# Attention over hyperedges: the feature sums of two chunks, and their use, in every second turn of the loop

## The chip, the core and the metric

The kernel runs on one core of one Trainium2 chip. A core has engines that run side by side, each with its own list of instructions that it works off in order: TensorE (PE in the profile; its weight loads are PEld), VectorE (DVE), ScalarE (ACT), GpSimd (POOL) and SyncE (SP), which here only issues transfers. An instruction that needs another engine's result waits on a semaphore, and everything behind it on the same engine waits too. The metric is the time of one execution on the device in microseconds (us), lower is better; given is the median of several runs.

## The reference, cut to what matters

Four graph layers run one after the other on x, 8 batches of 2048 nodes with 64 features. The change lies at the end of the first of them, where two candidates for a node, `industry` (from the adjacency matrix) and `g` (from the hyperedges), are weighed against each other and added to x:

```python
def attn_scores(f):
    return jnp.tanh(f @ fcW + fcb) @ av
...
industry = jnp.einsum('nm,bmf->bnf', adj / deg, x @ W_ind)
...
g = jnp.einsum('bne,benf->bnf', coefs1, all_he)
pair = jnp.stack([industry, g], axis=2)
coefs2 = jax.nn.softmax(attn_scores(pair), axis=-1)
out = jnp.einsum('bnk,bnkf->bnf', coefs2, pair)
...
# --- layer 0 (adj_preln) ---
h = jnp.maximum(_layernorm(x, axis=-1), 0.0)
x = x + _L0_gnn_ref(h, ...)
# --- layer 1 (adj_preln) ---
h = jnp.maximum(_layernorm(x, axis=-1), 0.0)
x = x + _L1_gnn_ref(h, adj, L1_gnn_W, L1_gnn_a)
```

A softmax over two scores is a sigmoid of their difference. So with d = score(industry) - score(g) the layer's output is g + (1 + tanh(d/2)) * (industry - g)/2, and that is how the kernel computes it.

## The kernel before, in words

The data lie transposed: two batches of 64 features fill the 128 partitions (a pair p, four of them), the 2048 nodes lie along the free axis in four chunks of 512. The stage of the change works through 4 pairs x 4 chunks = 16 chunks, numbered 0 to 15 (lines 1506 to 1592). Chunks 0 to 3 are pair 0, 4 to 7 pair 1, and so on. For each chunk i there are these steps:

- `fetch(i)`, line 1520: SP loads 256 KB of `industry` (half of it, already scaled) from DRAM into one of 8 buffers `iv`. It may only start when the buffer's last user, eight chunks earlier, is done.
- `first(i)` and `second(i)`, lines 1525 and 1528, both through `scores`, line 1509: TensorE multiplies the chunk of `iv`, or of `gT` (whose tiles are called `hn` in the profile), by fcW into a `pf` tile, one matmul per batch (two records each). There are two `pf` tiles. ScalarE takes the tanh into a `th_s` tile of 128x1024; six of these come from a pool named `pt`. `second` also has VectorE turn `iv` into (industry - g)/2 in place. That instruction overwrites what `first(i)` reads, so it waits for `first(i)` on TensorE.
- `differ(i)`, line 1534: VectorE subtracts the two tanh tiles, 128x1024.
- `third(i)`, line 1537: TensorE sums that difference over the features with weights av, one matmul per batch, into a `pd` tile; there are two of these. ScalarE takes the tanh in place. These are the feature sums of the title.
- `fourth(i)`, line 1545: VectorE computes (tanh + 1) * iv. For pair 0 it also adds g and x (two more instructions) and SP stores the result; for the other pairs GpSimd issues a transfer that adds the tile onto DRAM. After the last chunk of a pair, `late_tile` has GpSimd load one more megabyte of the adjacency matrix.

The turn i of the loop (line 1572) issues, in this order, `first(i+1)`, `second(i+1)`, `third(i-1)`, `differ(i)`, `fourth(i-2)`, `fetch(i+6)`; ahead of it stand `fetch(0)` to `fetch(6)`, `first(0)`, `first(1)` and `second(0)`. Between them `near(engine, i)` issues the steps that prepare pair 0 for the next layer's attention, by a plan that is written out by hand (`first_neighbours`, lines 1667 to 1794): in turns 4 to 8 and again 8 to 12 means, a layer norm and a projection (`mean`, `xc`, `q`, `ph`, `hS`, `raw`), in turns 12 to 14 a Newton iteration in small VectorE instructions, in turns 14 and 15 the spread of scores over partitions (`pb`, `R`), in turns 16 and 17 the first four `pt` tiles of the attention. The wrappers `V`, `A`, `G`, `S` and `kit.strict` keep the order of issue on each engine as the program has it.

The next layer's attention follows at once (`attend`, line 1821): VectorE makes two `pt` tiles of 128x1024 for each of 16 blocks of nodes, and TensorE multiplies them (`o`, `dn`).

Of the kernel before, what the change touches and what calls it, by code (L numbers as in the profile page):

```python
# [27 lines left out]
def half(b2):  # L28
    return slice(b2 * 64, (b2 + 1) * 64)


def cols(c, w=CW):
    return slice(c * w, (c + 1) * w)
# [603 lines left out]
class Kit:  # L637
# [97 lines left out]
    def mm(self, *args, **kw):  # L735

        one = self.nc.tensor.matmul(*args, **kw)  # L737
        if self.strict:
            self.tc.keep_in_program_order(one)
# [36 lines left out]
def layer0(kit, hn, x1_dram, open_early, late_tile, between):  # L776
# [542 lines left out]
    with ExitStack() as s0:  # L1319
# [125 lines left out]
        for j in range(last + 2 * NB):  # L1445
            i, k = divmod(j, NB)
# [55 lines left out]
    with ExitStack() as s0:  # L1502
        io = s0.enter_context(tc.tile_pool(name="o_io", bufs=1, reuse_waits="tile"))
        sb = s0.enter_context(tc.tile_pool(name="o_sb", bufs=2, reuse_waits="tile"))
        ps = s0.enter_context(tc.tile_pool(name="o_ps", bufs=2, space=PSUM, reuse_waits="tile"))
        chunks = [(p, c) for p in range(NP) for c in range(NCW)]
        ivs, ths, tgs, ccs, xs = {}, {}, {}, {}, []

        def scores(v, f):

            act = A if kit.strict else nc.scalar
            pf = ps.tile([P, 2, CW], FP, tag="pf", name="pf")
            for b2 in range(2):
                kit.strict = kit.strict or b2 == 1
                mm(pf[:, b2, :], fcW[half(b2), :], v[half(b2), :], start=True, stop=True)
            th = one.pt.tile([P, HN], FP, tag="pt", name="th_s").rearrange("p (b n) -> p b n", b=2)
            act.activation(th, pf, AF.Tanh, bias=fcb, scale=f)
            return th

        def fetch(i):  # L1520
            p, c = chunks[i]
            ivs[i] = io.tile([P, CW], FP, tag=f"iv{i % 8}", name="iv")
            S.dma_start(out=ivs[i], in_=ind_dram[p, :, cols(c)])

        def first(i):
            ths[i] = scores(ivs[i], 2.0)

        def second(i):
            p, c = chunks[i]
            tgs[i] = scores(gT[p][:, cols(c)], 1.0)  # L1530

            V.scalar_tensor_tensor(ivs[i], gT[p][:, cols(c)], -0.5, ivs[i], op0=OP.mult, op1=OP.add)

        def differ(i):
            V.tensor_sub(ths[i], ths[i], tgs.pop(i))

        def third(i):
            pd = ps.tile([P, CW], FP, tag="pd", name="pd")
            th = ths.pop(i)
            for b2 in range(2):  # L1540
                mm(pd[half(b2), :], Av, th[:, b2], start=True, stop=True)
            A.activation(pd, pd, AF.Tanh, scale=0.5)
            ccs[i] = pd

        def fourth(i):
            p, c = chunks[i]
            df = ivs.pop(i)
            V.scalar_tensor_tensor(df, ccs.pop(i), 1.0, df, op0=OP.add, op1=OP.mult)
            if p:
                G.dma_start(out=x1_dram[p, :, cols(c)], in_=df, accum_op=OP.add)  # L1550
            else:
                V.tensor_add(df, df, gT[p][:, cols(c)])
                V.tensor_add(xs[c], xs[c], df)
                nc.sync.dma_start(out=x1_dram[p, :, cols(c)], in_=xs[c])
            if c == NCW - 1:
                late_tile(p)

        G = InOrder(tc, nc.gpsimd)
        for i in range(5):
            fetch(i)  # L1560
        for c in range(NCW):
            xs.append(sb.tile([P, CW], FP, tag="x", name="xo", bufs=NCW))
            S.dma_start(out=xs[c], in_=t["xT"][0, :, cols(c)])
            if c < 2:
                fetch(5 + c)
        first(0)
        kit.strict = False
        first(1)
        second(0)
        near = one.first_neighbours(xs, V, A)  # L1570

        for i in range(len(chunks) + 2):
            near("DVE", i)
            if 0 < i < len(chunks) - 1:
                first(i + 1)
            if i < len(chunks) - 1:
                second(i + 1)
            near("PE0", i)
            if 0 < i <= len(chunks):
                third(i - 1)  # L1580
            near("PE", i)
            if i < len(chunks):
                differ(i)
            if i > 1:
                fourth(i - 2)
            if 0 < i and i + 6 < len(chunks):
                fetch(i + 6)
            near("V2", i)
            near("ACT", i)
            if i in (3, 7, 11):  # L1590
                p = 1 + i // 4
                G.dma_start(out=x1_dram[p], in_=gT[p], accum_op=OP.add)
# [721 lines left out]
def four_layers(  # L2314
# [13 lines left out]
    with ExitStack() as s:  # L2328
# [20 lines left out]
        def between(_):  # L2349
            ahead.append(Layer1(kit, x1, aT))  # L2350
            return ahead[0]

        layer0(kit, hn, x1, early, late_tile, between)
        later = []

# [56 lines left out]
```

## Time and profile before

| what | value |
|---|---|
| median of 3 runs | 1859.51 us (1858.75 to 1859.87) |
| the profiled execution: its own time | 1860.53 us |
| its span, first to last instruction | 1858.7 us |
| mean granted TensorE clock | 0.994 of full speed |
| first `pf` matmul of the stage | at 351.09 us |
| last `fourth` of the stage on VectorE | 420.99 to 421.67 us |
| 16 `differ` on VectorE | 1212 to 1225 ns each |
| 32 tanh of `scores` on ScalarE | 1106 to 1121 ns each |
| 64 `pd` matmul records of `third` | 592 to 643 ns each |
| 64 `pf<-iv` matmul records of `first` | 589 to 693 ns each |

The table has rows of the page and of the answers on single tiles. Times are counted from the start of the span. Records of TensorE overlap: two matmuls on different rows or columns of the array run at once, and the next starts while the last drains, so a record's duration is longer than the distance to the next one. In a row of the timeline the bracket at the end is the idle time of that engine just before the row, and what ended it.

### The profile page before, as it was taken

The page shows a single profiled execution, that of the slowest core. Times are in us where ns is not written, and L with a number is a line of the kernel's source. Part 1 is how long each engine was busy: PE and PEld are TensorE (multiplying, and loading weights), DVE is VectorE, ACT ScalarE, POOL GpSimd, SP SyncE. Part 2 cuts the span into 40 slices and gives each one's busy share as a digit, 9 for nine tenths or more (in the row PEclk, how much of TensorE's full clock was granted, in tenths as well). Part 3 has the DMA queues.
Part 4 walks back from the last instruction along what each step waited for, and adds up shares of the span by engine and source line. Part 5 has one row for each costly group of instructions (what it writes and reads, how often), then busy time and mean ns, then how long its engine had stood idle before and what let it go on. Part 6 is the DMA issues. An engine that isn't in the chain of part 4 may idle for free.

```text
span 1858.7 us, 26259 instructions
## 1 busy us (share of the span) xinstructions
PE 1819.8 (98%) x10358; PEld 1139.3 (61%) x10358; DVE 1196.4 (64%) x1881; ACT 474.6 (26%) x1085; POOL 315.9 (17%) x437
## 2 busy tenths in 40 slices
PE   8999999899999999999999999999999999999997
PEld 7878767343333333467765577855687755777653
DVE  7778799789999998942346822357523277424465
ACT  5433455572222221121311112301112101113000
POOL 3212487120000000000112200012100021101122
PEclk9999999999999999999999999999999999999998
DMA  6677494492222222142101022100122011221000
GB/s 193 175 214 217 126 283 120 114 213 75 59 54 52 64 58 58 46 94 74 51 5 36 22 69 63 35 24 22 48 63 63 12 28 32 61 58 51 5 20 13
DMA packets 84389, 142.61 MB, mean 77 GB/s; under 512 B 31752, under 2 KB 32008, under 8 KB 81520
## 3 DMA queue, kind: packets, MB, share of 16 engines
q1 hardware_dynamic: 62832, 79.59, 14.6%
q0 software_dynamic: 21200, 58.03, 12.8%
q10 hardware_dynamic: 224, 3.22, 0.5%
q8 instruction: 83, 1.36, 0.3%
q14 instruction: 50, 0.41, 0.1%
HBM read 106.85 MB, written 37.09 MB: 77 GB/s over the span
## 4 chain that ended last, share of the span: by engine, by line
PE 49%; issue 10%; DMA 2%; POOL 2%; DVE 1%; POOLq 0%; ACT 0%; SPq 0%; DVEq 0%
PE acc L737 31%; PE u L737 14%; PE py L737 2%; PE pv L737 1%; PE tv L744 1%; PE tx L744 1%; POOL fold L2298 1%; DMA den<-d_dram 0%; DMA xd<-e 0%; DMA d_dram<-ds 0%; DMA W3f<-in_L_gnn_weight 0%; PE tp L744 0%; POOL ot L2299 0%; DVE pt L1813 0%; POOL ot L2300 0%
## 5 line engine op out<-in xcount | busy, mean ns | idle before, releaser
L737 PE MATMUL acc<-aT,parts 128*128 128x512 f32 x1664 | 432.1, 404 | 0.0
L737 PEld LDWEIGHTS acc<-aT,parts 128*128 128x128 f32 x1664 | 305.2, 188 | 81.8 <-issue 23.1
L737 PE MATMUL o<-pt,hS 128*32 128x512 f32 x2048 | 247.5, 593 | 2.9 <-DVE pt L1813 1.6
L2286 DVE TENSOR_TENSOR pr<-u,embf 128x512 f32<-128x512 f32 x256 | 170.6, 687 | 120.6 <-PE u L737 114.0
L737 PE MATMUL u<-W3f,y 64*128 64x512 f32 x1024 | 241.3, 589 | 0.0
L1813 DVE SCALAR_TENSOR_TENSOR pt<-R,wd,aT 128x1024 f32<-128x1024 f32 x188 | 230.1, 1277 | 8.0 <-DMA R<-r_dram 5.7
L737 PEld LDWEIGHTS u<-W3f,y 64*128 64x128 f32 x1024 | 100.1, 187 | 119.6 <-issue 119.6
L737 PEld LDWEIGHTS o<-pt,hS 128*32 128x32 f32 x2048 | 75.0, 110 | 149.2 <-issue 124.3
L737 PE MATMUL dn<-pt,vd 128*32 128x512 f32 x1024 | 135.0, 593 | 0.0
L737 PE MATMUL u<-W3f,v 64*128 64x512 f32 x512 | 133.1, 596 | 0.0
L2298 POOL TENSOR_TENSOR fold<-fold 128x256 f32<-128x256 f32 x64 | 47.7, 746 | 477.0 <-DVE fold L2297 477.0
L2066 DVE TENSOR_TENSOR yb<-py,cb_f 128x512 f32<-128x512 f32 x32 | 22.1, 692 | 152.6 <-PE py L737 152.6
L1106 PE MATMUL acc<-at,Y 128*128 128x512 f32 x384 | 103.3, 405 | 0.0
L737 PE MATMUL acc<-aTl,parts 128*128 128x512 f32 x384 | 97.5, 396 | 0.0
L2175 POOL TENSOR_TENSOR bq<-bq,xp 128x512 f32<-128x512 f32 x16 | 20.6, 1288 | 423.0 <-ACT xp L2088 423.0
L2290 DVE TENSOR_TENSOR pr<-pr 128x512 f32<-128x512 f32 x128 | 88.0, 688 | 2.2
L737 PEld LDWEIGHTS u<-W3f,v 64*128 64x128 f32 x512 | 56.5, 186 | 48.6 <-issue 35.7
L1813 DVE SCALAR_TENSOR_TENSOR pt<-R,wd,aTl 128x1024 f32<-128x1024 f32 x64 | 79.3, 1280 | 8.7 <-PE dn L737 3.9
L737 PEld LDWEIGHTS acc<-aTl,parts 128*128 128x128 f32 x384 | 72.1, 188 | 17.0
L737 PEld LDWEIGHTS dn<-pt,vd 128*32 128x32 f32 x1024 | 38.2, 110 | 70.3 <-issue 55.6
L1106 PEld LDWEIGHTS acc<-at,Y 128*128 128x128 f32 x384 | 68.8, 188 | 12.7 <-issue 0.3
L2080 DVE TENSOR_TENSOR parts<-tp,parts 128x512 fp32r<-128x512 f32 x16 | 11.1, 691 | 85.2 <-ACT parts L2079 85.2
(372 smaller groups left out, 2709.8 us busy)
## 6 DMA issues: line engine op xcount, KB each, us to landing
at<-in_adjT POOLq DMA_DIRECT2D x32, 512.0 KB, 5.3
raw<-in_adjT SPq DMA_DIRECT2D x64, 256.0 KB, 3.4
aT<-in_adjT POOLq DMA_DIRECT2D x12, 1024.0 KB, 7.5
xp<-xd SPq DMA_DIRECT2D x45, 256.0 KB, 3.0
R<-r_dram SPq DMA_DIRECT2D x14, 512.0 KB, 3.7
hhi<-hi_dram POOLq DMA_DIRECT2D x18, 235.1 KB, 4.4
hlo<-lo_dram POOLq DMA_DIRECT2D x18, 235.1 KB, 4.6
hi_dram<-hi SPq DMA_DIRECT2D x16, 264.0 KB, 2.9
```

The costliest lines, as they stand in the source:

```text
L737: one = self.nc.tensor.matmul(*args, **kw)
L744: one = self.nc.tensor.transpose(dst, src, self.ident[0:k, 0:k])
L1106: mm(acc[p], Y[h][:, m, p, :], at[:, k, :], start=m + h == 0, stop=m == NT - 1 and h == 1)
L1813: V.scalar_tensor_tensor(pt, R, w, a.bitcast(FP), op0=OP.max, op1=OP.mult)
L2066: nc.vector.tensor_tensor(yb, py, bias[:, None, :].to_broadcast([P, 4, P]), op=OP.add)
L2080: nc.vector.tensor_tensor(lo, tp, hi.bitcast(FP), op=OP.subtract)
L2175: nc.gpsimd.tensor_add(bq, bq, xp)
L2286: nc.vector.tensor_tensor(a, u[h], emb[:, i, 8 * w : 8 * w + 8, None].to_broadcast([P, 8, F]), op=OP.mult)
L2290: nc.vector.tensor_add(pr[h], pr[h], a)
L2298: nc.gpsimd.tensor_add(fold[:, :, 0:2, :], fold[:, :, 0:2, :], fold[:, :, 2:4, :])
```

## The change

The loop's order is changed, and nothing else. `third` and `fourth` are issued for two chunks together in every even turn from 2 to 16, `third` now at the head of the turn ahead of `first(i+1)` and `second(i+1)`, and `fourth` at its old place after `differ(i)`. The loads are issued two at a time in the odd turns.

```diff
         for i in range(len(chunks) + 2):
             near("DVE", i)
+            if i and i % 2 == 0 and i <= len(chunks):
+                third(i - 2)
+                third(i - 1)
             if 0 < i < len(chunks) - 1:
                 first(i + 1)
             if i < len(chunks) - 1:
                 second(i + 1)
             near("PE0", i)
-            if 0 < i <= len(chunks):
-                third(i - 1)
             near("PE", i)
             if i < len(chunks):
                 differ(i)
-            if i > 1:
+            if i > 1 and i % 2 == 0:
                 fourth(i - 2)
-            if 0 < i and i + 6 < len(chunks):
-                fetch(i + 6)
+                fourth(i - 1)
+            for k in (i + 5, i + 6):
+                if i % 2 and 6 < k < len(chunks):
+                    fetch(k)
             near("V2", i)
             near("ACT", i)
             if i in (3, 7, 11):
```

Every chunk is still computed by the same instructions on the same engines. For an even chunk, `third` comes one turn later than before and `fourth` in the same turn; for an odd chunk, `third` comes in the same turn but ahead of the turn's other matmuls, and `fourth` one turn earlier. `fetch(7)` stays in turn 1, odd ones stay in their turns, and `fetch(8)`, `fetch(10)`, `fetch(12)` and `fetch(14)` move from the even turn to the odd one after it.

## The prediction

> **What bounds the kernel now.** I read the page first, then the busy time by stretches, then the timelines of TensorE and VectorE in the stage, each for its idle brackets.
>
> ```profile
> PE 1819.8 (98%) x10358; PEld 1139.3 (61%) x10358; DVE 1196.4 (64%) x1881; ACT 474.6 (26%) x1085; POOL 315.9 (17%) x437
> ```
>
> Over the whole span TensorE looks like the bound. But a share over stages with different limits does not price an edit in one of them, so I look at the stage (351 to 422 us) and at what follows.
>
> ```profile
> 420.00:430.00 10.00, 10.00 (x94) 3.56 (x89) 10.00 (x12) 1.95 (x3) 1.43 (x2) 1.00 0.74 181
> 470.00:700.00 230.00, 230.00 (x2108) 73.62 (x2104) 214.70 (x189) 53.09 (x160) 13.83 (x20) 1.00 0.23 56
> ```
>
> The columns are the stretch, its length, then busy time (instructions) of PE, PEld, DVE, ACT and POOL, the granted clock, DMA share and GB/s. Behind the stage VectorE is busy without a break (10.00 of 10.00) and then for 93% of the time. So a microsecond by which VectorE leaves the stage later is a microsecond at the end. VectorE's instructions in the stage are the same before and after; what can change is only how long it stands idle among them.
>
> ```profile
> 360.09 0.69 DVE L632 SCALAR_TENSOR_TENSOR iv<-hn,iv 128x512 f32<-128x512 f32 x1 [1.24 <-PE pf L737]
> 360.70 1.22 DVE L632 TENSOR_TENSOR th_s<-th_s 128x1024 f32<-128x1024 f32 x1
> 361.83 0.68 DVE L632 SCALAR_TENSOR_TENSOR iv<-pd,iv 128x512 f32<-128x512 f32 x1
> 362.55 0.69 DVE L632 TENSOR_TENSOR iv<-iv,hn 128x512 f32<-128x512 f32 x1
> 363.27 0.69 DVE L632 TENSOR_TENSOR xo<-xo,iv 128x512 f32<-128x512 f32 x1
> 363.89 0.68 DVE L632 SCALAR_TENSOR_TENSOR iv<-hn,iv 128x512 f32<-128x512 f32 x1
> ...
> 402.18 0.69 DVE L632 SCALAR_TENSOR_TENSOR iv<-hn,iv 128x512 f32<-128x512 f32 x1 [0.48 <-PE pf L737]
> 402.79 1.22 DVE L632 TENSOR_TENSOR th_s<-th_s 128x1024 f32<-128x1024 f32 x1
> 403.92 0.68 DVE L632 SCALAR_TENSOR_TENSOR iv<-pd,iv 128x512 f32<-128x512 f32 x1
> 404.52 0.17 DVE L632 TENSOR_SCALAR varn<-raw 128x32 f32<-128x32 f32 x1
> ...
> 407.35 0.68 DVE L632 SCALAR_TENSOR_TENSOR iv<-hn,iv 128x512 f32<-128x512 f32 x1
> ```
>
> This is VectorE's timeline. From start to start: the half-difference in `second` 0.61 us, `differ` 1.13, `fourth` 0.60, or 2.06 for pair 0 with its two additions. A turn of pair 0 is 3.80 (360.09 to 363.89). From 357 us, where the loop runs evenly, to 421.6 VectorE's brackets add up to 8.9 us: 1.24 early, then 2.04 in turns 7 and 8, 1.78 in turns 9 and 10, 3.01 in turns 11 and 12, 0.84 in turns 16 and 17.
>
> ```profile
> 401.00 1.13 PE L737 MATMUL pf<-iv,fcWf 64*128 64x512 f32 x4
> 401.96 1.02 PE L737 MATMUL pf<-hn,fcWf 64*128 64x512 f32 x4
> 402.92 1.08 PE L737 MATMUL pd<-th_s,Avf 128*64 128x512 f32 x4
> 403.93 1.13 PE L737 MATMUL pf<-iv,fcWf 64*128 64x512 f32 x4
> ...
> 414.66 1.94 PE L737 MATMUL pd<-th_s,Avf 128*64 128x512 f32 x8
> 416.53 1.05 PE L737 MATMUL o<-pt,hS 128*32 128x512 f32 x4
> ```
>
> TensorE's blocks follow each other by 0.96 (`first`), 0.96 (`second`) and 1.01 (`third`), 2.93 a turn. Its brackets between 351 and 422 add up to 4.1 us. So the stage is in balance: for pair 0 VectorE is slower (3.80 against 2.93), later TensorE. Neither stops the other for long, because `third(i-1)` has two other blocks (1.92 us) in front of it in its turn, during which VectorE can finish `differ(i-1)` and go on.
>
> **The change, part by part.** *Two blocks of `third` together.* Two apart take 2.02 (twice 1.01), two together 1.87 (414.66 to 416.53), so 0.15 is saved. `first` and `second` of two chunks now follow each other too; I give that 0.2, the two places where a 0.96 block is longer than the two 0.43 steps inside it. That is 0.35 a pair of chunks, 2.8 us for eight, and it counts only where TensorE sets the pace.
>
> *`third` ahead of `first` and `second`.* This is the new wait. In an even turn TensorE's list is `third(i-2)`, `third(i-1)`, `first(i+1)`. `third(i-1)` needs `differ(i-1)`, VectorE's last instruction of the turn before. Queued behind it on TensorE are `first(i+1)` and `second(i+1)`. VectorE's next instruction, the half-difference of `second(i+1)`, waits for `first(i+1)`, and behind that stand `differ(i)` and both `fourth`. So in every even turn VectorE finishes `differ(i-1)`, then waits for a round trip: 0.1 until TensorE starts, 1.01 for `third(i-1)`, 1.18 from the start of `first` to the instruction that waits for it (401.00 to 402.18): 2.3 us. The 1.92 us of cover is gone.
>
> Turn by turn, VectorE's stops: turns 2 and 4, nothing in front: 2.3 each. Turns 6 and 10: one clip of 0.3 from the neighbour plan fills part: 2.0 each. Turns 8 and 12: VectorE already waits there for projections (2.04 and 3.01 before). The new stop costs at least its 2.3 with the old ones inside it, at most 2.0 + 2.3 = 4.3; TensorE has two more blocks of `ph` of 1.87 each to run there, so I take 3.8. Turn 14: 0.8 of `rstd` and `hS` fill: 1.5. Turn 16: there is no `first`, but `fourth(15)` now stands before three `pt` and waits for its tanh: the old 0.84 and one more tanh step of 0.5, 1.3. Sum 19.0, against 8.9 before: **+10.1 us**; with the bounds for turns 8 and 12, +7.1 to +11.1.
>
> *`fourth` for two chunks.* Same instructions; for pair 0 they form a block of 4.1 us in turns 2 and 4, in front of the next `differ`. That makes a long stop on TensorE. After VectorE starts `second(3)` it needs 0.61 + 1.13 + 4.12 + 0.61 + 1.22 + 0.05 = 7.7 us until `third(3)` may start; TensorE meanwhile has 0.74 left of `second(3)`, 1.92 for chunk 4, 1.01 for `third(2)` and some 0.5 of waiting for a `pf` tile: 4.2. It stands 3.5 us. The same holds in turn 5, and in turn 13, where the Newton chain (404.52 to 407.35, 2.8 us) stands in front of `differ(13)`. These stops are part of VectorE's ledger above, but they touch the clock:
>
> ```profile
> 343.17 2.02 PE L737 MATMUL pgs<-mix,S 128*114 128x512 f32 x2 [3.37 <-DVE gn L632]
> ```
>
> ```profile
> 342.00:346.00 4.00, 2.83 (x8) 1.70 (x9) 1.62 (x3) 0.01 (x1) 0.00 (x0) 0.54 0.00 0
> 346.00:350.00 4.00, 3.70 (x8) 1.45 (x6) 0.26 (x1) 2.07 (x8) 0.00 (x0) 0.61 0.00 0
> ```
>
> The one stop of that length inside this kernel, 3.37 us before 343.17, is followed by 6.8 us at about half clock (0.54 and 0.61 in the two stretches). A round trip at half clock costs 2.2 more (1.01 + 1.18 again). With three stops that is 0 (no drop) to 6.6 (three drops on the path); a drop can begin too early or too late for the round trip, so I take half: **+3.3**.
>
> [...]
>
> *Loads two at a time.* Four loads start a turn later, none adds bytes. The work that hides them: `fetch(8)` landed 3.1 us after its issue at 364.41, its chunk was read at 378.80. The late ones wait anyway until the transfer that adds the buffer's old chunk to DRAM has landed (5 to 10 us). `fetch(12)` was issued at 385.96, took 9.5 and was read at 396.19, 0.7 us to spare. As the stage stretches, its reader moves back about as far as the load. I cost it at 0; without that cover each microsecond late is one on TensorE, at most some 2 per load. GpSimd's list keeps its order. ScalarE's work is 2.5 us a turn (twice 1.01 and 0.52), below TensorE's, in the new order too.
>
> The sum against the profiled span is 1858.7 + 13.4 = 1872.1. The median lies 0.8 above that span, so the time is 1859.5 + 13.4 = 1872.9.
>
> **The rivals.** *No clock drop, the round trips alone:* 1859.5 + 10.1 = 1869.6, down to 1866.6 if turns 8 and 12 hide more. For it: the stops are barely as long as the one that dropped. Against: there are three of them.
>
> *Faster: TensorE sets the pace.* If VectorE runs far enough ahead that `differ(i-1)` is always done, the 2.8 us saved on TensorE are the whole effect: 1856.7. For it: 98% busy, and 4.1 us of idle in the stage. Against: the half-difference cannot run ahead of `first`, and `differ(i-1)` stands behind it. It decides if the stops of the even turns stay under 1.1 us on average (8.9 over eight).
>
> *The loads come late.* With readers in pairs, chunks 12 and 14 could wait 2 us each, on top of the main case: 1877.
>
> *Absorbed, no change:* a later wait takes up the delay. Against: VectorE's waits between 418 and 480 us add up to 5 us only, so at most 5 of the 13 could vanish. It takes halved round trips as well.
>
> **How the numbers follow.** Round trips with clock drops 0.53, between 1870 and 1877; without drops 0.24; loads late 0.10; faster 0.06; no change 0.07. The predicted time is the first case's, 1873 rounded. The range takes the first two cases and the lower half of the loads: 1866 (+7.1) to 1878 (10.1 + 1.0 + 6.6 = +17.7, rounded up). About what a measurement can tell from no change is 0.2%, 3.7 us: faster 0.06, same 0.07, slower 0.87.
>
> **What would show it.** In the changed profile VectorE's `iv<-hn,iv` of odd chunks should carry brackets of about 2.3 us from PE `pf`, those of even chunks none. TensorE's `pd` rows should come as x8 or in twos, with waits of some 3.5 us for VectorE in turns 4, 6 and 14. The first `o` of the attention should start 10 to 14 us later, the granted clock should dip in the stage, and everything behind it should keep its length. I am wrong if the brackets are short, if TensorE shows no stops, or if the attention starts late and still ends on time.

## The result, and the profile after

The changed kernel takes 1874.41 us (median of 6 runs, 1871.80 to 1876.07), against 1858.90 us of six runs of the kernel before beside it: a ratio of 1.0082, with a 95% interval of 1.0072 to 1.0092. It is slower by 15.5 us; forecast were 13.4.

The profiled execution has a span of 1874.3 us, which is 15.6 more than before. The page's first part shows where it is not:

```profile
PE 1827.3 (97%) x10358; PEld 1143.0 (61%) x10358; DVE 1196.5 (64%) x1881; ACT 475.2 (25%) x1085; POOL 315.9 (17%) x437
```

VectorE is busy for as long as before (1196.4 there), with as many instructions. TensorE is busy 7.5 us longer with the same 10358 matmuls: some of them ran longer. Now the stage, from near its first matmul to near its end, and the 264 us behind it. First the changed kernel, then the kernel before; the columns are those of the prediction (the stretch, its length, busy time of PE, PEld, DVE, ACT and POOL, granted clock, DMA share, GB/s).

```profile
352.00:436.00 84.00, 71.70 (x316) 28.65 (x316) 56.98 (x91) 51.59 (x69) 15.32 (x19) 0.90 0.69 153
436.00:700.00 264.00, 263.83 (x2400) 85.64 (x2396) 244.10 (x219) 66.47 (x206) 13.82 (x20) 1.00 0.24 61
```

```profile
352.00:422.00 70.00, 65.92 (x330) 27.44 (x330) 57.50 (x92) 51.10 (x70) 14.07 (x18) 1.00 0.81 183
422.00:686.00 264.00, 263.37 (x2400) 85.79 (x2396) 245.08 (x219) 66.70 (x206) 15.22 (x22) 1.00 0.24 61
```

The stage is longer, VectorE does the same work in it, and the granted clock fell from 1.00 to 0.90. In the 264 us behind it the same 2400 matmuls run as before. Counted exactly, from the start of the first `pf` to the end of the fourth `pt` on VectorE, the stage went from 69.98 to 85.64 us (+15.66), and what lies behind it from 1437.7 to 1437.9. So the whole loss arose in the stage and arrived at the end in full. (One `fourth` of 0.60 us stands behind that point in the kernel before and ahead of it in the changed one; more on it below.)

VectorE's timeline shows in which turns. The rows are the half-difference in `second`, with the bracket that says how long VectorE stood idle before it, and one `differ` between them:

```profile
360.76 0.69 DVE L632 SCALAR_TENSOR_TENSOR iv<-hn,iv 128x512 f32<-128x512 f32 x1 [2.24 <-PE pf L737]
...
366.61 0.68 DVE L632 SCALAR_TENSOR_TENSOR iv<-hn,iv 128x512 f32<-128x512 f32 x1
367.21 1.22 DVE L632 TENSOR_TENSOR th_s<-th_s 128x1024 f32<-128x1024 f32 x1
372.51 0.69 DVE L632 SCALAR_TENSOR_TENSOR iv<-hn,iv 128x512 f32<-128x512 f32 x1 [4.09 <-PE pf L737]
...
385.23 0.69 DVE L632 SCALAR_TENSOR_TENSOR iv<-hn,iv 128x512 f32<-128x512 f32 x1 [3.52 <-PE pf L737]
...
394.70 0.69 DVE L632 SCALAR_TENSOR_TENSOR iv<-hn,iv 128x512 f32<-128x512 f32 x1 [2.35 <-PE pf L737]
...
424.07 0.69 DVE L632 SCALAR_TENSOR_TENSOR iv<-hn,iv 128x512 f32<-128x512 f32 x1 [3.25 <-PE pf L737]
```

These are odd chunks: VectorE waits for `first` in every even turn. The half-differences of even chunks, such as the one at 366.61, have no bracket. TensorE's timeline over the same turns shows the other half of the round trip:

```profile
363.99 1.08 PE L737 MATMUL pd<-th_s,Avf 128*64 128x512 f32 x4
368.48 1.98 PE L737 MATMUL pd<-th_s,Avf 128*64 128x512 f32 x4 [3.41 <-DVE th_s L632]
370.38 2.08 PE L737 MATMUL pf<-iv,fcWf 64*128 64x512 f32 x4
372.25 1.92 PE L737 MATMUL pf<-hn,fcWf 64*128 64x512 f32 x4
...
420.04 1.97 PE L737 MATMUL pd<-th_s,Avf 128*64 128x512 f32 x4 [3.31 <-DVE th_s L632]
421.94 2.08 PE L737 MATMUL pf<-iv,fcWf 64*128 64x512 f32 x4
423.81 1.92 PE L737 MATMUL pf<-hn,fcWf 64*128 64x512 f32 x4
```

`third(2)` runs at 363.99, then TensorE stands 3.41 us until VectorE's `differ(3)` (367.21 to 368.43) is done. `third(3)` and `first(5)` follow, each taking 1.9 us from its start to the next start where it took 0.96 to 1.01 before, and only then may VectorE go on (372.51). The busy time of TensorE by stretches, with the granted clock as the column after it, gives the reason:

```profile
364.35:367.76 3.41, 0.72 (x4) 1.00 0.27 100
367.76:374.59 6.83, 6.11 (x13) 0.50 0.38 103
378.00:381.41 3.41, 1.23 (x6) 1.00 0.68 185
381.41:384.82 3.41, 3.39 (x8) 0.50 0.89 297
415.55:418.96 3.41, 1.18 (x6) 1.00 0.96 193
418.96:425.79 6.83, 5.75 (x13) 0.50 0.76 210
```

There are three stretches of half clock, 17.1 us in all, where the stage had none before. Each begins inside a stop of TensorE or at its end, and so covers the round trip that the stop leads to.

### The profile page after: what moved, and what is told of

Same layout as the page of the kernel before. It is cut to its first block, busy times and chain, and to the rows that moved or that the text cites. A ratio compares the mean times of both kernels' runs of the same rounds, so it can differ in the third digit from the quotient of the medians.

```text
span 1874.3 us, 26254 instructions
## 1 busy us (share of the span) xinstructions
PE 1827.3 (97%) x10358; PEld 1143.0 (61%) x10358; DVE 1196.5 (64%) x1881; ACT 475.2 (25%) x1085; POOL 315.9 (17%) x437
## 4 chain that ended last, share of the span: by engine, by line
PE 49%; issue 10%; DMA 2%; POOL 2%; DVE 1%; POOLq 0%; ACT 0%; SPq 0%; DVEq 0%
PE acc L737 31%; PE u L737 14%; PE py L737 2%; PE pv L737 1%; PE tv L744 1%; PE tx L744 1%; POOL fold L2301 1%; DMA den<-d_dram 0%; DMA xd<-e 0%; DMA W3f<-in_L_gnn_weight 0%; DMA d_dram<-ds 0%; PE tp L744 0%; POOL ot L2302 0%; DVE pt L1816 0%; POOL ot L2303 0%
```

## The experiments

Eight kernels were run. Stage lengths are counted as above (69.98 before, 85.64 after); each median is compared with the kernel before as it was measured beside it, 1859.71 us for the first four and 1860.19 for the others. Edits are against the changed kernel or against the kernel before, as said.

**The pair moved back.** Against the changed kernel: `third` still takes two chunks, at its old place behind `first` and `second`.

```diff
-            if i and i % 2 == 0 and i <= len(chunks):
-                third(i - 2)
-                third(i - 1)
             if 0 < i < len(chunks) - 1:
                 first(i + 1)
...
             near("PE0", i)
+            if i and i % 2 == 0 and i <= len(chunks):
+                third(i - 2)
+                third(i - 1)
             near("PE", i)
```

> The changed kernel with the pair of thirds put back behind first and second (its old place in the turn), everything else of the change kept. Theory (the round trip from VectorE's differ through third and first back to VectorE is the cost, because third stands at the head): the two blocks in front of third cover differ again, so 1859 to 1862 us against 1858.9 before; VectorE's waits for the pf matmul in even turns are under 1.3 us each, TensorE has no wait over 2 us in the stage, the clock does not dip there. Rival (doing two chunks together is the cost, wherever it stands: a longer block of fourths, fewer chances to overlap): 1869 us or more, with the waits still there.

Measured: 1861.97 us, ratio 1.0008 (0.9998 to 1.0018), stage 71.78 us. TensorE's rows in turn 4:

```profile
366.52 1.08 PE L737 MATMUL pd<-th_s,Avf 128*64 128x512 f32 x4
367.98 1.08 PE L737 MATMUL pd<-th_s,Avf 128*64 128x512 f32 x4 [0.39 <-DVE th_s L632]
```

The wait of 3.41 us is down to 0.39, no half clock shows in the stage (its `pf<-iv` records last at most 693 ns, as before, where the changed kernel has up to 1220), and 13.9 of the 15.7 us of stage are gone. So nearly all of the cost comes from the place at the head of the turn. The pair, the pairs of `fourth` and the loads, all of which this kernel has, are left with 1.8 us of stage and 2.3 us of the medians together.

**The place alone.** Against the kernel before: `third(i-1)`, single as it was, moved to the head of its turn.

```diff
+            if 0 < i <= len(chunks):
+                third(i - 1)
             if 0 < i < len(chunks) - 1:
                 first(i + 1)
...
             near("PE0", i)
-            if 0 < i <= len(chunks):
-                third(i - 1)
             near("PE", i)
```

> The kernel before with one thing moved: third(i-1), one chunk a turn as before, to the head of the turn ahead of first and second; fourth and the loads as before. Theory (the place at the head costs, not the pairs): in every turn VectorE waits the 2.3 us of the round trip less what fourth(i-3) fills of it (2.06 for pair 0, 0.60 later), about 1.7 us in each of some eight turns beyond pair 0 in place of 8.9 us of waits before, about +10 us: 1867 to 1872. TensorE's single waits stay under 3 us. Rival (the pairing is the cost): 1859, no change.

Measured: 1869.97 us, ratio 1.0053 (1.0034 to 1.0073), stage 81.67 us. TensorE's rows, two turns of pair 0:

```profile
363.82 1.08 PE L737 MATMUL pd<-th_s,Avf 128*64 128x512 f32 x4 [1.67 <-DVE iv L632]
364.83 1.13 PE L737 MATMUL pf<-iv,fcWf 64*128 64x512 f32 x4
365.79 1.02 PE L737 MATMUL pf<-hn,fcWf 64*128 64x512 f32 x4
368.49 1.08 PE L737 MATMUL pd<-th_s,Avf 128*64 128x512 f32 x4 [1.67 <-DVE iv L632]
```

TensorE waits eight times for VectorE, 1.07 to 2.17 us at a time, and a turn of pair 0 lasts 4.67 us (363.82 to 368.49), where it lasted 3.80. The bracket names `iv` and not `th_s`: with two `pd` tiles, `third(i-1)` also needs the tile that `fourth(i-3)` reads, and that instruction stands right behind `differ(i-1)` on VectorE (367.75 to 368.43 in its timeline). So the round trip here is one instruction of VectorE longer than the one forecast, and it comes in nearly every turn: VectorE waits for `first` in twelve of them, 0.79 to 2.24 us at a time. The place alone, with that wait, costs 10.3 us by itself, against 15.5 for the whole change. One stretch of half clock, 3.4 us from 379.64 on, lies in it. How much of the 10.3 is the `pd` tile was not tried. Pairs make fewer round trips, eight in all, and longer ones.

**TensorE kept busy.** Against the changed kernel: in turns 4, 6 and 14 the matmuls of the even chunk's `third` are issued four times, into the same place and with the same result, so that TensorE works through the stop instead of standing still.

```diff
-                third(i - 2)
+                third(i - 2, 4 if i in (4, 6, 14) else 1)
                 third(i - 1)
...
-        def third(i):
+        def third(i, times=1):
...
-            for b2 in range(2):
+            for b2 in [0, 1] * times:
                 mm(pd[half(b2), :], Av, th[:, b2], start=True, stop=True)
```

> The changed kernel, with the even chunk's third matmuls issued four times over (the same result written again) in turns 4, 6 and 14, so that TensorE works during its three long waits instead of standing. Theory: the three dips of the granted clock vanish and with them the part of VectorE's waits that is above the 2.3 us round trip, some 5 us: 1868 to 1871 us against 1874.4, VectorE's waits in turns 4, 6 and 14 at 2.4, 2.1 and 1.6 us instead of 4.1, 3.5 and 3.3. Rival (the dips lie beside the path, and the longer waits have another cause): 1874 to 1877 us, longer by the added matmuls if anything.

Measured: 1871.53 us, ratio 1.0055 (1.0036 to 1.0073), stage 79.57 us. TensorE's rows in turn 4:

```profile
362.25 3.65 PE L737 MATMUL pd<-th_s,Avf 128*64 128x512 f32 x16
366.73 1.08 PE L737 MATMUL pd<-th_s,Avf 128*64 128x512 f32 x4 [0.83 <-DVE th_s L632]
367.74 1.13 PE L737 MATMUL pf<-iv,fcWf 64*128 64x512 f32 x4
368.70 1.02 PE L737 MATMUL pf<-hn,fcWf 64*128 64x512 f32 x4
```

Twelve matmul records more in each of three turns, and the stage is 6.1 us shorter. The added work fills the stop down to 0.83 us, the clock does not fall anywhere in the stage (1.00 granted from 352 to 430 us), and `third(3)` to `first(5)` takes 1.01 instead of 1.90. VectorE's brackets in turns 4, 6 and 14 are 2.24, 1.90 and 1.41 us instead of 4.09, 3.52 and 3.25: 5.3 less together. These waits came out within 0.2 us of what was expected, the median 0.5 us above it. This separates the two terms: without the halved clock the stage is 9.6 us longer than before, and the halved clock is worth 6.1 in the profiled executions. Of the medians it is worth less, 1874.41 - 1871.53 = 2.9, or 3.7 if each is first taken against the kernel before as measured beside it (15.5 and 11.8). Two things the records show bear on that. The profiled execution of the changed kernel, at a mean granted clock of 0.991, is the slowest of its six; the quickest, 1871.80 us, has 0.994, which is the clock of the profiled kernel before. That suggests that how much of the stage runs at half clock differs from run to run; only one execution was profiled, so it is not shown. And the profiled execution of this experiment needed 3.5 us more behind the stage than the changed kernel did; a stretch of half clock lies in that part (two `mean` records at 727.75 us take 1.07 us, two at 729.82 take 0.59), and how much of the 3.5 it makes was not separated.

**`differ` ahead of the new wait.** Against the changed kernel: `differ(i)` is issued ahead of `first(i+1)` and `second(i+1)`.

```diff
+            if i < len(chunks):
+                differ(i)
             if 0 < i < len(chunks) - 1:
                 first(i + 1)
...
             near("PE", i)
-            if i < len(chunks):
-                differ(i)
```

> The changed kernel with differ(i) issued ahead of first(i+1) and second(i+1) in every turn, third still at the head. Theory: VectorE then has one instruction of 1.13 us to do inside each round trip of 2.3 us, so seven waits shrink by about 1.1 us each (8 us), TensorE's long waits shrink below the 3.3 us that were followed by half clock (another 5 us), 1861 to 1865 us against 1874.4 for the changed kernel. Rival (the delay comes from the loads in twos, or from transfers that arrive late): 1874 as with the change.

Measured: 1864.51 us, ratio 1.0021 (1.0012 to 1.0031), stage 73.80 us. VectorE can now do `differ(i)` before it waits for `first(i+1)`, and the round trip opens: its stops for `first` in turns 4, 8 and 12 are 0.50, 1.22 and 1.22 us, where the changed kernel has 4.09, 2.35 and 2.35. TensorE still waits 1.68, 1.53 and 1.57 us at `third(i-1)` in turns 4, 6 and 14; no drop of the clock follows (the block behind each takes 1.08 us, where the changed kernel has 1.97 to 1.98). With the pair still at the head 4.8 of the 15.5 us are left: what costs is that VectorE's next work stood behind the wait.

**`fourth` alone in pairs.** Against the kernel before.

```diff
-            if i > 1:
+            if i > 1 and i % 2 == 0:
                 fourth(i - 2)
+                fourth(i - 1)
```

> The kernel before with nothing but fourth for two chunks in even turns; third single at its old place, loads as before. Theory: fourth(i-1) now waits in its own turn for third(i-1) and its tanh, some 0.5 us beyond pair 0, and the first block of 4.1 us makes TensorE wait once or twice: 1860 to 1862 us. Rival (the block of fourths alone delays differ enough to make the long TensorE waits and the clock dips): 1865 us or more.

Measured: 1865.03 us, ratio 1.0026 (1.0017 to 1.0036). That is more than expected, and the rival's number, but not by the rival's way: no long wait of TensorE and no half clock come from the block of 4.1 us (the `third` behind the first such block and the one behind the second take 1.08 us each, as before). The stage is 72.05 us, 2.1 longer: 0.6 is `fourth(15)`, which now stands ahead of the last three `pt` instead of behind them, and 1.5 is more idle time of VectorE, spread over turns 8 to 16. TensorE waits 1.06, 0.94 and 1.28 us at `third`, where the kernel before has two such waits, 0.62 and 0.98. The rest, 2.5 us, comes behind the stage. TensorE's rows at the start of the attention:

```profile
416.68 1.05 PE L737 MATMUL o<-pt,hS 128*32 128x512 f32 x4
419.98 2.78 PE L737 MATMUL o<-pt,hS 128*32 128x512 f32 x10 [2.24 <-DVE pt L632]
```

In turn 16 both `fourth` stand in front of the `pt` tiles that TensorE needs; it waits 2.24 us instead of 1.15, and 3.4 us of half clock begin at 419.84, so that the ten records that took 1.48 us take 2.78. The expectation had left out that a pair at the end of the loop delays the next stage's first tiles. About 1.5 us of the 2.5 stand there; the remainder arises more than 300 us later and is not explained.

**The loads alone in twos.** Against the kernel before.

```diff
-            if 0 < i and i + 6 < len(chunks):
-                fetch(i + 6)
+            for k in (i + 5, i + 6):
+                if i % 2 and 6 < k < len(chunks):
+                    fetch(k)
```

> The kernel before with nothing but the loads two at a time in odd turns. Theory: they are covered, 1859 us, no change within 1.5 us; at most chunk 12 or 14 makes TensorE wait 2 us. Rival (late loads are part of the 15.5 us): 1861 us or more, with first of an even chunk waiting for a transfer.

Measured: 1860.27 us, ratio 1.0005 (0.9996 to 1.0014), stage 70.33 us, 0.35 longer. There is one new wait of TensorE, a short one, at `first(12)` for its load:

```profile
396.25 1.13 PE L737 MATMUL pf<-iv,fcWf 64*128 64x512 f32 x4 [0.27 <-DMA iv<-ind_dram]
```

Four loads a turn later cost nothing that the medians show. The 0.7 us that the forecast counted as spare for `fetch(12)` were not quite enough here.

**`differ` first, alone.** Against the kernel before: one step is moved, nothing is paired.

```diff
+            if i < len(chunks):
+                differ(i)
             if 0 < i < len(chunks) - 1:
                 first(i + 1)
...
             near("PE", i)
-            if i < len(chunks):
-                differ(i)
```

> The kernel before with only differ(i) issued ahead of first(i+1) and second(i+1); nothing in pairs. Theory: VectorE does differ while it would wait for first, so some of its 8.9 us of waits close: about 1 us below the kernel before, 1857 to 1858.5. It tells how much of a gain in the version with pairs comes from the pairs. Rival: differ now stands in front of the half-difference and delays it, 1859 to 1861.

Measured: 1858.64 us, ratio 0.9996 (0.9987 to 1.0004). The stage is 1.3 us shorter (68.69): VectorE no longer waits for `first`, where the kernel before has brackets of 1.24, 0.48, 0.38 and 0.48 us from 357 us on, while some of its other waits are longer. Behind the stage 0.8 us are given back. It can't be told from the kernel before.

**All that helped, together.** The changed kernel with the pair moved back as in the first experiment, `differ` first, and `fourth` in pairs in the odd turns:

```diff
-            if i > 1 and i % 2 == 0:
-                fourth(i - 2)
-                fourth(i - 1)
+            if i > 2 and i % 2:
+                fourth(i - 3)
+                fourth(i - 2)
```

> A version meant to keep what the pairing saves on TensorE: third for two chunks behind first and second in even turns, differ(i) ahead of first(i+1), both fourths one turn later in the odd turn (so that no fourth waits for its tanh), loads in twos. Theory: no round trip and fewer changes between the two kinds of matmul: 1.5 to 3 us below the kernel before, 1856 to 1857.5. Rival (the stage is limited by VectorE's own work in a way that the order cannot help): 1859 or above.

Measured: 1860.39 us, ratio 1.0014 (1.0000 to 1.0027); not faster, so the expectation failed. The stage did become shorter, 68.21 against 69.98 us, but what lies behind it took 1440.2 instead of 1437.7. Of both, 0.6 us is only the order: `fourth(14)` too now stands behind the fourth `pt`. So the stage gained 1.2 us, and what lies behind lost 1.9. Of that, 1.1 us stands at two places 400 us behind the stage, where TensorE waits for ScalarE's `v`. First this kernel, then the kernel before:

```profile
820.49 1.16 PE L737 MATMUL py<-Wxc,v 128*128 128x128 f32 x8 [1.00 <-ACT v L2233]
830.48 1.16 PE L737 MATMUL py<-Wec_f,v 128*128 128x128 f32 x8 [1.50 <-ACT v L2235]
```

```profile
822.15 1.16 PE L737 MATMUL py<-Wxc,v 128*128 128x128 f32 x8 [0.45 <-ACT v L2230]
831.58 1.16 PE L737 MATMUL py<-Wec_f,v 128*128 128x128 f32 x8 [0.93 <-ACT v L2232]
```

The brackets are 2.50 us together against 1.38. Why `v` comes later there was not tried, and runs of the kernel before differ among themselves by 7 us (1855.97 to 1863.09), so a gain of 1.2 us in one stage is within what single executions scatter. No version tried is faster than the kernel before by more than the scatter.

## Why the prediction was right

**The bound.** That VectorE's idle time in the stage sets the end, and that nothing behind takes the delay up, held: +15.66 us in the stage, +0.2 behind it.

**The round trip and the ledger.** The mechanism is shown from both sides: with the place alone a loss of 10.3 us comes, without it all but 2.3 goes. VectorE's idle brackets turn by turn, in us; the last column is the experiment in which TensorE was kept busy:

| turn | forecast | changed kernel | TensorE kept busy |
|---|---|---|---|
| 2 | 2.3 | 2.24 | 2.24 |
| 4 | 2.3 | 4.09 | 2.24 |
| 6 | 2.0 | 3.52 | 1.90 |
| 8 | 3.8 | 3.49 | 3.50 |
| 10 | 2.0 | 1.81 | 1.82 |
| 12 | 3.8 | 3.50 | 3.51 |
| 14 | 1.5 | 3.25 | 1.41 |
| 16 | 1.3 | 1.92 | 1.26 |
| sum | 19.0 | 23.8 | 17.9 |

The price of 2.3 us was right to within 0.1 where the clock was whole. With the clock whole, each turn lies within 0.3 us of its forecast; turns 8 and 12, where the bounds were wide, came 0.3 below the value taken. (The bounds for turn 12 had been built with turn 8's 2.04 us; with its own 3.01 they are 3.0 to 5.3, and the 3.50 lies in them too.) The sum there is 17.9 - 8.9 = +9.0, where +10.1 was forecast; its stage was longer by 9.6. The difference is one instruction. The forecast took VectorE's work in the stage to be the same, but `fourth(15)`, which follows the fourth `pt` in the kernel before, now stands ahead of the last three, and TensorE waits for those tiles. The kernel before, then the changed kernel:

```profile
417.39 3.68 DVE L632 SCALAR_TENSOR_TENSOR pt<-R,wd,aT 128x1024 f32<-128x1024 f32 x3 [0.30 <-ACT R L632]
420.99 0.68 DVE L632 SCALAR_TENSOR_TENSOR iv<-pd,iv 128x512 f32<-128x512 f32 x1
```

```profile
432.13 0.69 DVE L632 SCALAR_TENSOR_TENSOR iv<-pd,iv 128x512 f32<-128x512 f32 x1 [0.17 <-ACT pd L632]
432.74 3.67 DVE L632 SCALAR_TENSOR_TENSOR pt<-R,wd,aT 128x1024 f32<-128x1024 f32 x3
```

Idle time and this 0.6 make 9.0 + 0.6 = 9.6 with TensorE kept busy, and 14.9 + 0.6 = 15.5 of the 15.66 in the changed kernel.

**The clock.** Forecast was +3.3, half of the 6.6 that three drops on the path would cost; the half was a hedge that no row gave. In the profiled execution all three came and each fell on its round trip: against the last column, turns 4, 6 and 14 are longer by 1.85, 1.62 and 1.84 us and turn 16, for which `second(15)` at half clock makes TensorE late, by 0.66: 6.0 together. So the miss of this execution (+15.6 against +13.4) is made up of the clock, set 2.7 too low, the 0.6 of `fourth(15)` that was left out, and the round trips, set 1.1 too high. Over the medians the clock is worth 2.9 to 3.7 us by the experiment, so that the hedge came out near; there the miss (+15.5 against +13.4) lies mostly in the rest, +11.8 where +10.1 was forecast, and was not taken apart. The stops of TensorE ahead of the three drops were 3.41, 2.20 and 3.31 us, where three of 3.5 had been forecast; the second is shorter because half clock had made TensorE itself late (`second(5)` ended at 374.17 at half clock). The forecast rested on one stop of 3.37 us that was followed by half clock; that the clock fell in turn 6 too, after 2.20 us, was luck for it.

**What counted for nothing.** The loads: 0 forecast, 0.1 of the medians measured, and in the changed kernel `first` never waits for one. The view of the `iv` tile's matmuls there:

```profile
its engine sat idle before it (us, times) until:
  ACT th_s L632: 1.0, 3
who waited for it (us, times):
  DVE iv L632: 21.1, 9
```

The first two lines say what TensorE waited for before `first`: ScalarE, 1.0 us, and no transfer. The last says that VectorE waited 21.1 us for it, 4.6 before. The 0.35 us a pair saved on TensorE was counted only where TensorE sets the pace; with the pair at its old place the stage does not get shorter (71.78), so it is not seen.

**What was missed.** `fourth` in pairs has a price of its own: alone it made the kernel 4.8 us slower, 2.1 in the stage and the rest behind it. The forecast had given it 0.5 us, in turn 16, and a part in the stops of TensorE. In the kernel with the pair moved back, which has those pairs too, only 2.3 us are left. How much of the changed kernel's 15.5 us the pairs of `fourth` make, beyond the 0.6 above, was not separated.

## What to carry to other kernels

Before a step is moved ahead on an in-order engine, ask what its input is and what stands behind it: if the other engine's next instruction waits for that, the distance between the two was cover, and the price is one round trip for every time the step is issued (here 2.24 us in turns 2 and 4 with the clock whole). Grouping work on one engine made the other engine's stops fewer and longer here (VectorE waited for `first` in seven turns, 1.27 to 4.09 us at a time, where the place alone has twelve of 0.79 to 2.24). Stops of TensorE cost twice here, once as waiting and again as half clock just when its work is on the path: the stage was 9.6 us longer with the clock whole, and 6.1 more with the half clock that came with stops of 3.41, 2.20 and 3.31 us. If a gain in one stage is no larger than the scatter of the kernel's runs, look for it at the end of the span before believing it.

## What the runs showed of the hardware

The clock did not fall by the length of one stop alone. In the changed kernel a stop of 2.20 us was followed by half clock; with the place alone a stop of 1.82 us was (it ended at 378.14, half clock began at 379.64), and one of 2.17 us that ended at 418.37 was not. What the drops of the changed kernel's stage share is a grid: they begin at 367.76, 381.41 and 418.96 us, 13.65 and 37.55 us apart, 4 and 11 times 3.41, and last 3.41 or 6.83 us. Each follows a cell of this grid with little matmul work in it: 0.72, 1.23 and 1.18 us of 3.41 in the changed kernel's stretches above. Two cells of the kernel with the place alone, and the one behind the second:

```profile
365.99:369.40 3.41, 1.74 (x8) 1.00 0.46 154
376.23:379.64 3.41, 1.59 (x8) 1.00 0.27 71
379.64:383.05 3.41, 3.41 (x11) 0.50 0.75 221
```

A cell with 1.74 us of matmuls (51%) was not followed by half clock, one with 1.59 us (47%) was. The five drops met in the stages (three in the changed kernel, one with the place alone, one with `fourth` alone in pairs, whose cell has 1.30 us) follow cells that are 21 to 47% busy. Elsewhere in the span this does not hold: in the kernel before a cell with 2.85 us of small matmuls (84%, 205.78 to 209.19) is followed by half clock (0.50 to 212.60). So the busy time of the records is not the whole measure, and what is stays open.
